# Attention and mixture of experts on one core: the experts' products in pairs

## The chip, the cores and the metric

The kernel runs on one core of one Trainium2 chip. The metric is device time in microseconds (us). Three runs of the kernel before took 2577.6, 2577.72 and 2578.16; the median is 2577.72.

## The reference

Everything is float32. The input x (4 x 1024 x 1024) is normalised per token to xn, and the result is the sum of x and two branches of xn:

```
x  = layernorm(x)                                    # xn
q, v = xn @ Wq, xn @ Wv                              # 16 heads
state[t] = sigmoid(beta) * state[t-1] + v[t]
y  = layernorm(q * state) * ln_g + ln_b
attn = (y * silu(xn @ Wg)) @ Wo                      # the projection

# 64 experts of 384 hidden units, 8 per token, at most 128 tokens each
h   = silu(xg[e] @ w1[e].T) * (xg[e] @ v1[e].T)      # xg[e]: 128 tokens gathered for e
ffn = scatter_add(weight * (h @ w2[e]))
out = x + attn + ffn
```

What changes is the order of the second half of the kernel, in which the 64 experts and the projection with Wo are computed. No value that is computed changes.

## The kernel before

The first half (to about 1232 us of the span) normalises, routes, scans and gates; it leaves the gated rows in DRAM (`gated`, 16 units of 256 rows), the tokens in `rows`, and x in the output `out`. The second half is `Experts.run`: a loop over 64 experts, with the projection's units cut into steps between them. The TensorE (PE) order, and that of VectorE (DVE) and ScalarE (ACT), is the order of the program there: `in_order(self.tc, ORDERED)` ties each instruction to the one before on its engine. SyncE (SP) issues loads and GpSimd (POOL) issues gathers and adds to `out`; each of these queues works through its own instructions in order, though a scheduler may place them earlier than the program text.

**Products of an expert, `hidden(e)`.** The hidden layer is a 2 x 2 block product done with seven block products (Winograd's form of Strassen's method). It needs sums of the left blocks (S1 to S4 in `s`, from `left_sums`, four additions of 128 x 256) and of the weights' blocks (T3, T1 by `sums31`, T2, T4 by `sums24`, each 128 x 1536; T1 is made in place in the weights). A block has 64 tokens, so the products use half of the PE array's columns, two at a time (`both`, with `tile_position` 0 or 64), in four groups:

1. into bank C, with S3 x T3 and S4 x B22,
2. into bank A, with A11 x B11 and S1 x T1,
3. into banks D and B, with S2 x T2 and A12 x B21,
4. into banks B and A, with A22 x T4 (half as long).

After each group ACT copies banks to SBUF and DVE adds them up in `q`, `up` and `act`; ACT applies silu, and DVE's last product leaves the hidden values in `act`. In between DVE makes the sums for the next expert and turns its gathered tokens (`turned`, a transpose from `xg` into `xgT`).

**Output of an expert.** `turn_hidden(e)` transposes `act` with three full-width matmuls into bank T, and ACT copies it to `hT`. `output(e)` computes y in two halves of 512 columns (banks D and T, three matmuls each), ACT scales them into a fresh tile `ys`, and POOL adds `ys` to the rows of `out` by an indirect DMA (L1001). The weights w2 of the expert (1.5 MB, one slot) are loaded by SP after the output before has used the slot.

**Steps of the projection, `steps`.** A unit has seven steps of four full-width matmuls each: step 1 into bank a (then an ACT copy), 2 into b, 3 into c (DVE adds b to the copy first, `c11`; ACT copies c), 4 adds to a (ACT copies it), 5 adds to c (DVE: `c12`, after which the row block `olo` is added to `out` by POOL), 6 adds to a (DVE: `c22`, L178, which reads bank a), 7 adds to a again (ACT copies it, and `ohi` is added to `out`). The projection's banks a, b and c are others than the experts' A, B and C. A unit's left factors come by `load_gated` and get their own `left_sums` on DVE; there is one place for them, so the next unit is loaded when step 7 has read it.

**The order.** For each expert e: `turn_hidden(e-1)`, `hidden(e)`, `output(e-1)`, then one or two steps, in the pattern 2, 2, 2, 1. So PE goes from full width to half columns and back once for each expert. The weights w and v of expert e+2 are loaded, and its tokens gathered, after `hidden(e)` (`fetch`). Each float32 matmul leaves two records in the trace, so a step is eight records and y twelve.

Of the kernel before, what the change touches and what calls it, by code (L numbers as in the profile page):

```python
# [39 lines left out]


NSLOT = 7


BLOCKS = ((0, 0), (1, 0), (1, 1), (0, 1))
# [774 lines left out]
class Experts:  # L820
# [8 lines left out]
    def load(self, e, n):  # L829


        if e >= E:
            return
        pools, (w, k) = self.pools, self.ws[n]
        slot = (n, e % 2) if n < 2 else (0, e % 2 ^ 1) if e == E - 1 else n
        if slot not in self.slots:
            t = (pools.x if e == 0 and n < 2 else pools.y)(f"w{n}_{e}")
            self.slots[slot] = t.rearrange("p a b -> p (a b)")
        t = self.slots[slot]
        done = self.nc.sync.dma_start(out=t, in_=w[e])  # L840
        if (e, n) == (1, 1):
            self.tc.keep_in_program_order(done)
        self.weights[e, n] = t.rearrange("p (k f) -> p k f", k=k)

    def fetch(self, e):

        for n in (1, 0):
            self.load(e, n)
        self.gather(e)

    def gather(self, e):
        if e >= E:
            return
        nc, pools = self.nc, self.pools
        if self.xg is None:
            self.xg = pools.block("xg").rearrange("p k (x c) -> p (k x) c", c=DQ)
        for r in range(NQ):
            nc.gpsimd.indirect_dma_start(  # L858
                out=self.xg[:, e % 2 * NQ + r, :],
                out_offset=None,  # L860
                in_=self.rows.rearrange("n (q c) -> (n q) c", q=NQ),
                in_offset=bass.IndirectOffsetOnAxis(ap=self.part[:, r, e : e + 1], axis=0),
            )
        nc.gpsimd.indirect_dma_start(
            out=self.wt[:, e % NQ, :],
            out_offset=None,
            in_=self.wtab,
            in_offset=bass.IndirectOffsetOnAxis(ap=self.idx[:, e : e + 1], axis=0),
        )

    def places(self):


        pools = self.pools
        t = pools.left.tile([P, NSLOT, KH, P], F32, tag="w", name="t23")
        t = t.rearrange("p a b c -> p (a b c)")
        u = pools.block("t4").rearrange("p a b -> p (a b)")
        n = KH * F
        self.t2, self.t3, self.t4 = (
            v.rearrange("p (k f) -> p k f", f=F) for v in (t[:, 0:n], t[:, n : 2 * n], u[:, 0:n])  # L880
        )
        self.p6, self.q = t[:, 2 * n : 2 * n + F], u[:, n : n + F]
        self.s = pools.one.tile([P, 4, KH, TH], F32, tag="cur", name="s")

    def turned(self, e):

        if e >= E:
            return
        xT = self.pools.line.tile([P, KD, P], F32, tag="line", name=f"xgT_{e}")
        done = self.nc.vector.transpose(  # L890
            xT.rearrange("p k (r i) -> p k r i", i=Q),
            self.xg[:, e % 2 * NQ : (e % 2 + 1) * NQ].rearrange("p r (k j) -> p k r j", j=Q),
        )
        if e == 0:
            self.tc.keep_in_program_order(done)
        self.xTs[e] = xT

    def left_sums(self, e):


        if e >= E:
            return
        vector = self.nc.vector
        a11, a12, a21, a22 = self.left_blocks(e)
        s1, s2, s3, s4 = (self.s[:, i] for i in range(4))
        vector.tensor_tensor(s3, a11, a21, ALU.subtract)
        vector.tensor_tensor(s1, a21, a22, ALU.add)
        vector.tensor_tensor(s2, s1, a11, ALU.subtract)
        vector.tensor_tensor(s4, a12, s2, ALU.subtract)

    def left_blocks(self, e):
        xT = self.xTs[e]
        return [xT[:, k : k + KH, i : i + TH] for i in (TH, 0) for k in (0, KH)]

    def right_blocks(self, e):

        return [self.weights[e, n][:, k : k + KH] for n in range(2) for k in (0, KH)]

    def sums31(self, e):

        if e < E:
            b11, _, b12, b22 = self.right_blocks(e)
            self.nc.vector.tensor_tensor(self.t3, b22, b12, ALU.subtract)  # L923
            self.nc.vector.tensor_tensor(b12, b12, b11, ALU.subtract)

    def sums24(self, e):
        if e < E:
            _, b21, t1, b22 = self.right_blocks(e)
            self.nc.vector.tensor_tensor(self.t2, b22, t1, ALU.subtract)  # L929
            self.nc.vector.tensor_tensor(self.t4, b21, self.t2, ALU.subtract)  # L930

    def hidden(self, e):


        nc, pools = self.nc, self.pools
        a11, a12, _, a22 = self.left_blocks(e)
        b11, b21, t1, b22 = self.right_blocks(e)
        s1, s2, s3, s4 = (self.s[:, i] for i in range(4))
        ba, bb, bc, bd = (self.banks[n][:, 0:F] for n in "ABCD")
        lo, hi = slice(0, TH), slice(TH, P)  # L940

# [12 lines left out]

        every, q, r, s = range(KH), self.q, self.act, self.p6
        both((bc, s3, self.t3, every), (bc, s4, b22, every))
        self.sums31(e + 1)
        both((ba, a11, b11, every), (ba, s1, t1, every))  # L960
        nc.scalar.copy(q, ba)
        nc.scalar.copy(r[lo], ba[hi])
        nc.scalar.copy(r[hi], ba[lo])
        nc.vector.tensor_tensor(q, bc, q, ALU.add)
        up = pools.scratch.tile([P, SH], F32, tag="sc", name=f"up_{e}")[:, 0:F]
        nc.vector.tensor_tensor(up, q, r, ALU.add)
        both((bd, s2, self.t2, every), (bb, a12, b21, every))
        nc.scalar.copy(s[hi], bd[lo])
        nc.scalar.copy(s[lo], bd[lo])
        nc.vector.tensor_tensor(up, up, s, ALU.add)  # L970
        nc.vector.tensor_tensor(q[lo], q[lo], s[lo], ALU.add)
        both((bb, a22, self.t4, (0, 1)), (ba, a22, self.t4, (2, 3)))
        nc.scalar.copy(r[lo], ba[hi])
        nc.vector.tensor_tensor(r, bb, r, ALU.add)
        nc.vector.tensor_tensor(r[lo], r[lo], q[lo], ALU.add)
        nc.scalar.activation(r, r, AF.Silu)
        self.turned(e + 1)
        nc.vector.tensor_tensor(r, r, up, ALU.mult)
        self.left_sums(e + 1)
        self.sums24(e + 1)  # L980
        for n in range(2):
            del self.weights[e, n]

    def turn_hidden(self, e):
        nc, pt = self.nc, self.banks["T"][:, 0:F].rearrange("p (j i) -> p j i", i=P)
        for j in range(KF):
            nc.tensor.transpose(pt[:, j, :], self.act[:, j * P : (j + 1) * P], self.ident)
        nc.scalar.copy(self.hT, pt)  # L988

    def output(self, e):  # L990
        nc, pools = self.nc, self.pools
        w2, wt, hT = self.weights.pop((e, 2)), self.wt[:, e % NQ, e : e + 1], self.hT
        ys = pools.line.tile([P, D], F32, tag="line", name=f"ys_{e}")
        for h, cols in enumerate((H0, H1)):
            ps = self.banks["DT"[h]]
            for j in range(KF):
# [45 lines left out]
    def begin(self, idx, part):  # L1042
        self.idx, self.part = idx, part
        v = self.pools.line.tile([P, S], F32, tag="line", name="act")
        self.act, self.hT = v[:, 0:F], v[:, F : 2 * F].rearrange("p (j i) -> p j i", i=P)
        self.wt = v[:, 2 * F :].rearrange("p (x e) -> p x e", e=E)
        self.fetch(0)

    def turn_first(self):
        self.places()  # L1050
        self.turned(0)
        self.left_sums(0)
        self.sums31(0)

    def run(self):
        nc, pools, units = self.nc, self.pools, B * NM
        self.banks = {n: pools.bank(tag, [P, SH], f"h{n}") for n, tag in zip("ABCDT", "abcrt")}
        with in_order(self.tc, [mybir.EngineType.SP]):
            self.load(1, 1)
            self.load_wo()  # L1060
            self.load(1, 0)
            gated = self.load_gated(0)
            self.load(0, 2)
        self.gather(1)
        wo_sums = right_sums(nc.vector, self.wo_b, lambda n: pools.block(f"wo_{n}"))


        plan = [(u, n) for u in range(units - 2) for n in (2, 2, 2, 1)]
        plan += [(units - 2, n) for n in (2, 2, 1, 1, 1)] + [(units - 1, 1)] * 3
        u, todo = -1, None  # L1070
        with in_order(self.tc, ORDERED):
            self.sums24(0)
            for _ in range(2):
                next(wo_sums)
            for e in range(E):
                if e > 0:
                    self.turn_hidden(e - 1)
                self.hidden(e)
                self.fetch(e + 2)
                if e == E - 2:  # L1080
                    self.load(E - 1, 2)
                if e == 0:
                    for _ in wo_sums:
                        pass
                else:
                    self.output(e - 1)
                    if e < E - 1:
                        self.load(e, 2)
                new, many = plan[e]
                if new > u:  # L1090
                    u, todo = new, self.project(new, gated)
                for _ in range(many):
                    next(todo, None)
                if e + 1 < E and plan[e + 1][0] > u:
                    gated = self.load_gated(u + 1)
            self.turn_hidden(E - 1)
            self.output(E - 1)
            for _ in todo:
                pass

# [47 lines left out]
```

## Time and profile before

| | |
|---|---|
| median of three runs | 2577.72 us |
| the profiled execution | 2577.84 us |
| its span, first to last instruction | 2576.1 us |
| granted TensorE clock | 0.999 |
| stage of experts and projection | about 1232 us to the end |
| DMA in all | 593.25 MB, of which SP's queue 448.03 and POOL's 143.72 |

The page of a profile lists the busy time of each engine, the busy shares over time, the DMA queues, the chain of work that ended last, and the costliest groups of instructions. A view by windows gives the same busy times for a stretch, with the share of time in which the 16 DMA engines were busy. The timeline lists single instructions or merged runs of them by start and duration; in brackets stands the idle time before one and what ended it. A matmul's duration in these records overlaps the next one's, so the distance of two starts is what a matmul costs.

### The profile page before, as it was taken

Reading aid. Unit: us, or ns where it says so; the run is one execution under the profiler, and the core shown is the slowest. Engines: PE = TensorE matmul, PEld = TensorE weight load, DVE = VectorE, ACT = ScalarE, POOL = GpSimd, SP = SyncE. Lnnn points to the kernel's source line nnn. Section 1 sums busy time; section 2 is a strip of 40 time slices with the busy share of each in tenths; the row PEclk is TensorE's granted clock in tenths of the full one; section 3 lists DMA queues with packets and bytes.
Section 4 is the critical chain, followed back from the end, with each engine's and each line's share of the span. In section 5 each row is a group of like instructions: output and inputs, shape, how many; then the busy total and the mean of one; then the engine's idle time right before and its main releaser. Section 6 shows DMA issues by size and latency. Waiting matters only on the chain.

```text
span 2576.1 us, 23153 instructions
## 1 busy us (share of the span) xinstructions
PE 2558.7 (99%) x8453; PEld 1132.6 (44%) x8453; DVE 1707.2 (66%) x2116; ACT 616.1 (24%) x1048; POOL 855.5 (33%) x630
## 2 busy tenths in 40 slices
PE   9999999999999999999999999999999999999998
PEld 5444444444444444444444444444444444444443
DVE  7946677375954668347866666666676666766673
ACT  4112212131111310112222222222222222222222
POOL 1452302101022010322344444444444444444441
PEclk9999999999999999999999999999999999999999
DMA  5655625543345442235899888898989899888995
GB/s 186 259 171 216 200 78 182 185 129 120 118 151 196 143 143 86 100 126 204 296 312 307 287 298 306 310 306 284 326 300 311 284 319 307 301 297 288 318 339 119
DMA packets 122354, 593.25 MB, mean 230 GB/s; under 512 B 15856, under 2 KB 52720, under 8 KB 89216
## 3 DMA queue, kind: packets, MB, share of 16 engines
q1 hardware_dynamic: 81488, 448.03, 47.0%
q0 software_dynamic: 40320, 143.72, 20.8%
q8 instruction: 67, 1.10, 0.2%
q14 instruction: 47, 0.39, 0.0%
q10 hardware_dynamic: 432, 0.01, 0.0%
HBM read 483.67 MB, written 124.81 MB: 236 GB/s over the span
## 4 chain that ended last, share of the span: by engine, by line
PE 95%; DVE 4%; issue 0%; DMA 0%; ACT 0%; POOLq 0%; SPq 0%; DVEq 0%
PE pa_g L143 9%; PE pa_o L143 8%; PE pa_q L143 7%; PE pa_v L143 7%; PE hD L997 7%; PE hC L946 7%; PE hA L946 7%; PE hT L997 6%; PE hD L946 6%; PE pc_o L143 4%; PE pc_g L143 4%; PE pc_v L143 4%; PE pc_q L143 4%; PE hB L946 3%; PE pb_o L143 2%; PE pb_g L143 2%
## 5 line engine op out<-in xcount | busy, mean ns | idle before, releaser
L858 POOL DMA_INDIRECT xg<-rows,tables x256 | 390.8, 1527 | 426.7 <-DVE xgT L890 363.3
L923 DVE TENSOR_TENSOR t<-w 128x1536 f32<-128x1536 f32 x64 | 112.5, 1758 | 236.7 <-PE hC L946 226.6
L143 PE MATMUL pa_g<-xT,w 128*128 128x512 f32 x512 | 230.8, 593 | 0.0
L143 PE MATMUL pa_q<-xT,w 128*128 128x512 f32 x480 | 216.6, 593 | 4.0 <-DVE y L178 4.0
L143 PE MATMUL pa_v<-xT,w 128*128 128x512 f32 x480 | 215.8, 592 | 0.0
L997 PE MATMUL hD<-w,act 128*128 128x512 f32 x384 | 181.9, 610 | 0.8 <-ACT act L988 0.7
L946 PE MATMUL hC<-t,s 128*64 128x384 f32 x512 | 179.1, 492 | 0.0
L946 PE MATMUL hC<-w,s 128*64 128x384 f32 x512 | 179.0, 492 | 0.0
L946 PE MATMUL hA<-w,xgT 128*64 128x384 f32 x512 | 175.6, 486 | 0.0
L946 PE MATMUL hD<-t,s 128*64 128x384 f32 x512 | 175.6, 486 | 0.0
L946 PE MATMUL hA<-w,s 128*64 128x384 f32 x512 | 175.6, 486 | 0.0
L946 PE MATMUL hB<-w,xgT 128*64 128x384 f32 x512 | 175.6, 486 | 0.0
L997 PE MATMUL hT<-w,act 128*128 128x512 f32 x384 | 175.2, 592 | 0.0
L143 PE MATMUL pa_o<-wo_T,gated 128*128 128x512 f32 x384 | 172.7, 592 | 0.8 <-DVE ohi L178 0.8
L691 POOL DMA_DIRECT2D gated<-y x64 | 48.6, 764 | 325.7 <-DVE y L686 315.4
L143 PEld LDWEIGHTS pa_g<-xT,w 128*128 128x128 f32 x512 | 96.8, 190 | 122.8 <-issue 121.8
L1001 POOL DMA_INDIRECT out_dram<-ys,tables x64 | 112.6, 1760 | 110.3 <-issue 49.5
L143 PEld LDWEIGHTS pa_q<-xT,w 128*128 128x128 f32 x480 | 90.5, 190 | 117.0 <-issue 109.8
L143 PEld LDWEIGHTS pa_v<-xT,w 128*128 128x128 f32 x480 | 91.1, 190 | 115.0 <-issue 110.0
L930 DVE TENSOR_TENSOR t<-w,t 128x1536 f32<-128x1536 f32 x64 | 112.5, 1759 | 7.4 <-DVE t L929 0.5
L143 PE MATMUL pc_g<-xT,w 128*128 128x512 f32 x256 | 115.7, 592 | 0.0
L143 PE MATMUL pc_q<-xT,w 128*128 128x512 f32 x256 | 115.5, 593 | 0.0
(245 smaller groups left out, 4414.9 us busy)
## 6 DMA issues: line engine op xcount, KB each, us to landing
w<-in_w_dram SPq DMA_DIRECT2D x128, 1536.0 KB
w<-in_v_dram SPq DMA_DIRECT2D x64, 1536.0 KB
w<-wsum SPq DMA_DIRECT2D x36, 1792.0 KB
wsum<-w POOLq DMA_DIRECT2D x12, 1792.0 KB
x<-in_x_dram SPq DMA_DIRECT2D x32, 512.0 KB
rows<-x POOLq DMA_DIRECT2D x32, 512.0 KB
gated<-y POOLq DMA_DIRECT2D x64, 256.0 KB
gated<-gated SPq DMA_DIRECT2D x16, 1024.0 KB
```

The costliest lines, as they stand in the source:

```text
L143: nc.tensor.matmul(ps, lhsT=lhs[:, slot, k, :], rhs=blocks[right][:, k, :], start=start and k == 0, stop=stop and k == KH - 1, skip_group_ ...
L691: nc.gpsimd.dma_start(out=gated[b, :, :, slot, m, :].rearrange("u p j -> p u j"), in_=yc[:, h * SH : (h + 1) * SH].rearrange("p (u j) -> p ...
L858: nc.gpsimd.indirect_dma_start(out=self.xg[:, e % 2 * NQ + r, :], out_offset=None, in_=self.rows.rearrange("n (q c) -> (n q) c", q=NQ), in ...
L923: self.nc.vector.tensor_tensor(self.t3, b22, b12, ALU.subtract)
L930: self.nc.vector.tensor_tensor(self.t4, b21, self.t2, ALU.subtract)
L946: nc.tensor.matmul(bank[half], lhsT=a[:, ks[k], :], rhs=b[:, ks[k], :], start=(k == 0), stop=(k == len(ks) - 1), tile_position=(0, half.st ...
L997: nc.tensor.matmul(ps, lhsT=hT[:, j, :], rhs=w2[:, j, cols], start=(j == 0), stop=(j == KF - 1))
L1001: nc.gpsimd.indirect_dma_start(out=self.out, out_offset=bass.IndirectOffsetOnAxis(ap=self.idx[:, e : e + 1], axis=0), in_=ys, in_offset=No ...
```

## The change

The experts are taken in groups: expert 0 alone, then pairs (1, 2), (3, 4) up to (61, 62), then 63 alone. In a group the products of both experts come first, one `hidden` after the other. Then for each expert of the group in turn: its transposes, one or two steps of the projection (`between`), and its y. Some groups have steps ahead of the first transposes (`ahead`) or at the end (`behind`). To have two experts at once, `s`, `act` and `xgT` have two places each; `ys` and `up` have one place for all experts. The transposes go into bank D instead of T. Within a pair the second expert's weight sums are made during the first's products, one by one (`right_sum`); those for the next group's first expert follow between the transposes and y. w2 is loaded in two halves of its columns, each as soon as y has used that half of the slot. The weight column `wt` has eight places. Gathers run four experts ahead.

```
+    def right_sum(self, e, n):
+        if e >= E:
+            return
+        b11, b21, b12, b22 = self.right_blocks(e)
+        to, a, b = {
+            3: (self.t3, b22, b12),
+            1: (b12, b12, b11),
+            2: (self.t2, b22, b12),
+            4: (self.t4, b21, self.t2),
+        }[n]
+        self.nc.vector.tensor_tensor(to, a, b, ALU.subtract)
...
     def load(self, e, n):
...
+        if n == 2:
+            from_ = w[e].rearrange("p (k f) -> p k f", k=k)
+            for cols in (H0, H1):
+                self.nc.sync.dma_start(out=t[:, :, cols], in_=from_[:, :, cols])
+            return
...
+    def more_places(self):
+        pools = self.pools
+        t = pools.line.tile([P, S], F32, tag="line", name="s1")
+        self.s[1] = t.rearrange("p (i k c) -> p i k c", i=4, k=KH)
+        self.ys = pools.line.tile([P, D], F32, tag="line", name="ys")
+        t, u = (pools.scratch.tile([P, SH], F32, tag="sc", name=n) for n in ("act1", "up"))
+        self.acts[1], self.up = t[:, 0:F], u[:, 0:F]
...
-    def hidden(self, e):
+    def hidden(self, e, turn, then_next):
...
-        self.sums31(e + 1)
+        if then_next:
+            for n in (3, 1):
+                self.right_sum(e + 1, n)
...
+        if then_next:
+            self.right_sum(e + 1, 2)
         both((bb, a22, self.t4, (0, 1)), (ba, a22, self.t4, (2, 3)))
...
-        self.turned(e + 1)
+        self.turned(turn)
         nc.vector.tensor_tensor(r, r, up, ALU.mult)
-        self.left_sums(e + 1)
-        self.sums24(e + 1)
+        if then_next:
+            self.right_sum(e + 1, 4)
...
     def turn_hidden(self, e):
-        nc, pt = self.nc, self.banks["T"][:, 0:F].rearrange("p (j i) -> p j i", i=P)
+        nc, pt = self.nc, self.banks["D"][:, 0:F].rearrange("p (j i) -> p j i", i=P)
...
     def run(self):
...
             self.load(1, 1)
             self.load_wo()
+            self.load(0, 2)
+            gated = self.load_gated(0)
             self.load(1, 0)
-            gated = self.load_gated(0)
-            self.load(0, 2)
...
+        plan = [((0,), 2, (1,), 0), ((1, 2), 0, (1, 2), 1)]
+        plan += [((e, e + 1), 0, (1, 2), e // 2 % 2) for e in range(3, last - 4, 2)]
+        plan += [((e, e + 1), 0, (1, 1), 0) for e in (last - 4, last - 2)]
+        plan += [((last,), 1, (0,), 0)]
...
+            for group, ahead, between, behind in plan:
+                new = group[-1] + 1
+                for e in group:
+                    self.hidden(e, e + 2 if e else 1, e != group[-1])
+                    for n in (1, 0):
+                        self.load(e + 2, n)
+                    if e == last - 1:
+                        self.load(last, 2)
+                    if e == group[0]:
+                        self.gather(e + 4 if e else 3)
+                project(ahead)
+                for i, e in enumerate(group):
+                    self.turn_hidden(e)
+                    project(between[i])
+                    if i == 0:
+                        if e == 0:
+                            for _ in wo_sums:
+                                pass
+                            self.turned(2)
+                        for n in (0, 1):
+                            self.left_sums(new + n)
+                        for n in (3, 1):
+                            self.right_sum(new, n)
+                    self.output(e)
+                    if e + 1 < last:
+                        self.load(e + 1, 2)
+                    if i == 0:
+                        self.gather(group[-1] + 4)
+                    if e == group[-1]:
+                        for n in (2, 4):
+                            self.right_sum(new, n)
+                project(behind)
```

`project(n)` here runs the next n steps of the projection, starts the next unit when one is done, and issues its load.

More of the change, by code (lines that the diff above doesn't have):

```diff
@@ L42 @@
 NSLOT = 7
+NWT = 8
 BLOCKS = ((0, 0), (1, 0), (1, 1), (0, 1))
@@ L838, in load @@
             self.slots[slot] = t.rearrange("p a b -> p (a b)")
-        t = self.slots[slot]
-        done = self.nc.sync.dma_start(out=t, in_=w[e])
+        t = self.weights[e, n] = self.slots[slot].rearrange("p (k f) -> p k f", k=k)
+        if n == 2:
[3 more added lines that the diff above has]
+            return
+        done = self.nc.sync.dma_start(out=self.slots[slot], in_=w[e])
         if (e, n) == (1, 1):
             self.tc.keep_in_program_order(done)
[L843 to L849, printed above, removed]
     def gather(self, e):
@@ L864, in gather @@
         nc.gpsimd.indirect_dma_start(
-            out=self.wt[:, e % NQ, :],
+            out=self.wt[:, e % NWT, :],
             out_offset=None,
@@ L882, in places @@
         self.p6, self.q = t[:, 2 * n : 2 * n + F], u[:, n : n + F]
-        self.s = pools.one.tile([P, 4, KH, TH], F32, tag="cur", name="s")
+        self.s = {0: pools.one.tile([P, 4, KH, TH], F32, tag="cur", name="s")}
+    def more_places(self):
[5 more added lines that the diff above has]
+        self.acts[1], self.up = t[:, 0:F], u[:, 0:F]
     def turned(self, e):
@@ L888, in turned @@
             return
-        xT = self.pools.line.tile([P, KD, P], F32, tag="line", name=f"xgT_{e}")
+        if e < 2:
+            self.xTs[e] = self.pools.line.tile([P, KD, P], F32, tag="line", name=f"xgT_{e}")
+        xT = self.xTs[e % 2]
         done = self.nc.vector.transpose(
@@ L895, in turned @@
             self.tc.keep_in_program_order(done)
-        self.xTs[e] = xT
     def left_sums(self, e):
@@ L904, in left_sums @@
         a11, a12, a21, a22 = self.left_blocks(e)
-        s1, s2, s3, s4 = (self.s[:, i] for i in range(4))
+        s1, s2, s3, s4 = (self.s[e % 2][:, i] for i in range(4))
         vector.tensor_tensor(s3, a11, a21, ALU.subtract)
@@ L911, in left_blocks @@
     def left_blocks(self, e):
-        xT = self.xTs[e]
+        xT = self.xTs[e % 2]
         return [xT[:, k : k + KH, i : i + TH] for i in (TH, 0) for k in (0, KH)]
@@ L917, in right_blocks @@
         return [self.weights[e, n][:, k : k + KH] for n in range(2) for k in (0, KH)]
[L919 to L930, printed above, removed]
-    def hidden(self, e):
-        nc, pools = self.nc, self.pools
+    def right_sum(self, e, n):
[10 more added lines that the diff above has]
+    def hidden(self, e, turn, then_next):
+        nc = self.nc
         a11, a12, _, a22 = self.left_blocks(e)
         b11, b21, t1, b22 = self.right_blocks(e)
-        s1, s2, s3, s4 = (self.s[:, i] for i in range(4))
+        s1, s2, s3, s4 = (self.s[e % 2][:, i] for i in range(4))
         ba, bb, bc, bd = (self.banks[n][:, 0:F] for n in "ABCD")
@@ L953, in both @@
                     )
-        every, q, r, s = range(KH), self.q, self.act, self.p6
+        every, q, r, s, up = range(KH), self.q, self.acts[e % 2], self.p6, self.up
         both((bc, s3, self.t3, every), (bc, s4, b22, every))
-        self.sums31(e + 1)
+        if then_next:
+            for n in (3, 1):
+                self.right_sum(e + 1, n)
         both((ba, a11, b11, every), (ba, s1, t1, every))
@@ L964, in hidden @@
         nc.vector.tensor_tensor(q, bc, q, ALU.add)
-        up = pools.scratch.tile([P, SH], F32, tag="sc", name=f"up_{e}")[:, 0:F]
         nc.vector.tensor_tensor(up, q, r, ALU.add)
@@ L984, in turn_hidden @@
     def turn_hidden(self, e):
-        nc, pt = self.nc, self.banks["T"][:, 0:F].rearrange("p (j i) -> p j i", i=P)
+        nc, pt = self.nc, self.banks["D"][:, 0:F].rearrange("p (j i) -> p j i", i=P)
         for j in range(KF):
-            nc.tensor.transpose(pt[:, j, :], self.act[:, j * P : (j + 1) * P], self.ident)
+            nc.tensor.transpose(pt[:, j, :], self.acts[e % 2][:, j * P : (j + 1) * P], self.ident)
         nc.scalar.copy(self.hT, pt)
     def output(self, e):
-        nc, pools = self.nc, self.pools
-        w2, wt, hT = self.weights.pop((e, 2)), self.wt[:, e % NQ, e : e + 1], self.hT
-        ys = pools.line.tile([P, D], F32, tag="line", name=f"ys_{e}")
+        nc, ys, hT = self.nc, self.ys, self.hT
+        w2, wt = self.weights.pop((e, 2)), self.wt[:, e % NWT, e : e + 1]
         for h, cols in enumerate((H0, H1)):
@@ L1044, in begin @@
         v = self.pools.line.tile([P, S], F32, tag="line", name="act")
-        self.act, self.hT = v[:, 0:F], v[:, F : 2 * F].rearrange("p (j i) -> p j i", i=P)
-        self.wt = v[:, 2 * F :].rearrange("p (x e) -> p x e", e=E)
-        self.fetch(0)
+        self.acts = {0: v[:, 0:F]}
+        self.hT = v[:, F : 2 * F].rearrange("p (j i) -> p j i", i=P)
+        self.wt = self.pools.small.tile([P, NWT, E], F32, tag="sel", bufs=1, name="wt")
+        for n in (1, 0):
+            self.load(0, n)
+        self.gather(0)
     def turn_first(self):
@@ L1052, in turn_first @@
         self.left_sums(0)
-        self.sums31(0)
+        for n in (3, 1):
+            self.right_sum(0, n)
     def run(self):
@@ L1060, in run @@
             self.load_wo()
+            self.load(0, 2)
+            gated = self.load_gated(0)
             self.load(1, 0)
-            gated = self.load_gated(0)
-            self.load(0, 2)
-        self.gather(1)
+        for e in (1, 2):
+            self.gather(e)
         wo_sums = right_sums(nc.vector, self.wo_b, lambda n: pools.block(f"wo_{n}"))
-        plan = [(u, n) for u in range(units - 2) for n in (2, 2, 2, 1)]
-        plan += [(units - 2, n) for n in (2, 2, 1, 1, 1)] + [(units - 1, 1)] * 3
@@ L1070, in run, with project @@
-        u, todo = -1, None
+        last = E - 1
+        plan = [((0,), 2, (1,), 0), ((1, 2), 0, (1, 2), 1)]
+        plan += [((e, e + 1), 0, (1, 2), e // 2 % 2) for e in range(3, last - 4, 2)]
+        plan += [((e, e + 1), 0, (1, 1), 0) for e in (last - 4, last - 2)]
+        plan += [((last,), 1, (0,), 0)]
+        todo, u, left = None, 0, 0
+        def project(n):
+            nonlocal todo, u, left, gated
+            for _ in range(n):
+                if left == 0:
+                    todo, left = self.project(u, gated), NSLOT
+                next(todo, None)
+                left -= 1
+                if left == 0:
+                    u += 1
+                    gated = self.load_gated(u) if u < units else None
@@ L1071, in run @@
         with in_order(self.tc, ORDERED):
-            self.sums24(0)
+            for n in (2, 4):
+                self.right_sum(0, n)
             for _ in range(2):
                 next(wo_sums)
[L1075 to L1095, printed above, removed]
@@ L1096, in run @@
-            self.turn_hidden(E - 1)
-            self.output(E - 1)
+            self.more_places()
+            for group, ahead, between, behind in plan:
+                new = group[-1] + 1
+                for e in group:
+                    self.hidden(e, e + 2 if e else 1, e != group[-1])
+                    for n in (1, 0):
+                        self.load(e + 2, n)
[14 more added lines that the diff above has]
+                            self.left_sums(new + n)
+                        for n in (3, 1):
+                            self.right_sum(new, n)
[5 more added lines that the diff above has]
+                    if e == group[-1]:
+                        for n in (2, 4):
+                            self.right_sum(new, n)
+                project(behind)
```

## The prediction

> **What bounds the kernel now.** I read the table of cores first (one core, 2576.1 us, granted clock 0.999, so no throttling), then the busy table and the chain of waits, then one window of the expert stage.
>
> ```profile
> PE 2558.7 (99%) x8453; PEld 1132.6 (44%) x8453; DVE 1707.2 (66%) x2116; ACT 616.1 (24%) x1048; POOL 855.5 (33%) x630
> PE 95%; DVE 4%; issue 0%; DMA 0%; ACT 0%; POOLq 0%; SPq 0%; DVEq 0%
> 1500.00:2000.00 500.00, 499.90 (x2036) 219.88 (x2034) 341.86 (x426) 138.44 (x264) 231.23 (x156) 1.00 0.89 304
> ```
>
> PE is never idle in the stage that changes (499.90 of 500), and the chain is 95% PE. So a microsecond added to or taken from PE's sequence is a microsecond of the kernel. The last two columns matter as well: the DMA engines are 0.89 busy at 304 GB/s, so transfers have little room to bunch.
>
> "Busy" hides the spacing of the matmuls, which the timeline of PE shows (start, duration, engine, line, tile):
>
> ```profile
> 1704.32 3.60 PE L143 MATMUL pa_o<-wo_T,gated 128*128 128x512 f32 x8
> 1707.75 0.49 PE L987 MATMUL hT<-ident,act 128*128 128x128 f32 x3
> 1708.17 0.54 PE L946 MATMUL hC<-t,s 128*64 128x384 f32 x1
> ...
> 1708.55 0.49 PE L946 MATMUL hC<-t,s 128*64 128x384 f32 x1
> ...
> 1708.87 0.49 PE L946 MATMUL hC<-t,s 128*64 128x384 f32 x1
> ...
> 1716.93 0.49 PE L946 MATMUL hB<-t,xgT 128*64 128x384 f32 x1
> ...
> 1717.35 2.84 PE L997 MATMUL hD<-w,act 128*128 128x512 f32 x6
> 1720.03 2.74 PE L997 MATMUL hT<-w,act 128*128 128x512 f32 x6
> 1722.61 3.60 PE L143 MATMUL pa_o<-wo_T,gated 128*128 128x512 f32 x8
> ```
>
> Half-column products start every 0.323 us, full-width matmuls every 0.429, transposes every 0.109. At the seam into half columns the last transpose takes 0.202 instead of 0.109 (+0.093), and the first product 0.374 instead of 0.323 (+0.051). At the seam out, the last product takes 0.416 instead of 0.316 (+0.100), and the first six matmuls of y take 2.68 instead of 2.58 (+0.105). One visit to half columns thus costs **0.349 us**; an expert with one step takes 18.29 us, of which the matmuls alone explain 17.94.
>
> **Part 1, experts in pairs.** The two orders of PE show 65 entries into half columns before and 34 after, so 31 visits go: 31 x 0.349 = 10.8 us. The seam out now meets a 128-column transpose. No row shows it; between nothing saved and the whole 0.105 saved on the 33 groups (0 to 3.5 us), I take half, as at the seam in (0.051): 1.6. Together **-12.4**.
>
> Does the pair hold without gaps? With hidden() of the first expert at 0, its groups start at 0, 2.6, 5.2, 7.8 and end at 9.1; the second's run from 9.1 to 18.2. DVE, by the rows of L923 to L978: T3 and T1 of the second expert from 2.8 to 6.4, adds, T2 at 10.0 to 11.7 (needed at 14.3), last adds and the transpose, T4 at 14.3 to 16.1 (needed at 16.9). That fits, with 0.8 us to spare. ACT copies hT of the first expert after the second's silu, at 20.8 to 21.3; one step of the projection (18.7 to 22.1) lies over it, so y starts at 22.1 without a wait. Cost nothing; without that step 2.6 us a pair.
>
> **Part 2, the steps between.** The plan now does 1 and 2 (and 1 behind) in one pair, 1 and 2 in the next. The order of PE shows what this makes of the seven steps: (1 | 2,3 | 4), then (5 | 6,7). Steps 6 and 7 both use bank a: step 7 may accumulate only when VectorE has read step 6's sum (L178). Before, an expert's products stood between them, except in the tail, which shows the price:
>
> ```profile
> 2560.38 3.60 PE L143 MATMUL pa_o<-wo_T,gated 128*128 128x512 f32 x8
> 2564.76 3.70 PE L143 MATMUL pa_o<-wo_T,gated 128*128 128x512 f32 x8 [0.79 <-DVE ohi L178]
> 2564.01 0.69 DVE L178 TENSOR_TENSOR ohi<-pa_o,sc_o 128x512 f32<-128x512 f32 x1 [2.67 <-PE pa_o L143]
> ```
>
> Eight matmuls at 0.429 are 3.43; the distance is 4.38, so 0.95 lost. VectorE is free in time (by my timetable its sums end at 29.7, step 6 at 31.2), so no more is lost. The order has 15 such neighbours, 1 before: 14 x 0.95 = **+13.3**. Behind the waiting matmul stand y and everything after; nothing passes it.
>
> **Part 3, the start.** Expert 0 stays alone. Between its products and those of expert 1, VectorE now has, after 1243.4: left sums of gated (2.5), the add after step 2 (ends 1247.9), two sums of Wo (rows L70, L73: 4.5), a transpose (1.2), eight left sums (3.1), T3 (1.8): 1258.5. PE gets there at 1255.9 (transposes 1247.0, 0.33, a step 3.43, y 5.14). Wait 2.6; T1, T2, T4 then chase it, some 0.3 more: **+2.9** (0 to 4). On SP the load of w for expert 1 moves behind w2 and gated into the slot whose last store ends near 1241; at the 0.43 MB a microsecond that the queue moves when alone it has landed by about 1250, and T1 reads it at 1258: nothing. The gather of the weight column moves behind the ys add and is used two pairs later: nothing.
>
> **Part 4, one place for ys; w2 in halves.** PE's own work is unchanged, but two transfers get deadlines.
>
> ys: ScalarE may write y of the second expert (at 38.2) only when the scatter-add of the first has landed, and PE feels it when bank D is not free for the next pair's third group (45.8, so landing by 45.0). The adds onto out wait for each other:
>
> ```profile
> POOL out_dram L1029 <- DMA out_dram<-ys,tables: 44.1, 10, 8.3
> POOL out_dram L1001 <- DMA out_dram<-ohi: 27.7, 7, 4.3
> ```
>
> In the second pair of each unit POOL issues both gathers (until about 29), then the projection's row block, then ys. By the trace's landing events from 1300 to 2500, a row block lands 12.0 us (olo) or 10.6 us (ohi) after issue, ys 6.8 (median; 13.7 at the 90th percentile): 29.1 + 12.0 + 6.8 = 47.9, 2.9 too late, 14 times: 41 us. The Trainium skill (DMA: Bandwidth & Descriptors, "Anatomy of one DMA — SWDGE (gpsimd) path") fits such a transfer by 2.0 us plus bytes over 436e3: 3.2 us for 512 KB. With 1.6 us for each issue both land by 38.7, and the wait is nothing. In the tail, with idle queues, the trace has 4.6 (olo) and 5.4 (ys), giving 39. The 12.0 was measured behind fresh 12 KB packets of w and v (0.46 us each); here 2 KB packets of w2 (0.084 us) compete, so I go nearer to the tail: 0.5 us x 14 = **+7**.
>
> w2: the second expert's halves are issued when the first expert's y lets go (25 and 27.5), queued behind w and v of the expert after next (issued at 14.6 and 17.2 on the same SP queue), and needed at 34.5 and 37.1. In the window, v took 7.4 us to land, w 10.8 (so until about 28) and a whole w2 8.6, beside the gathers. From 28, two halves of 2.0 us of engine time, sharing with the adds, land between 31 and 36. Between no wait and 1.5 us I take 0.4 x 14 = **+6**. The load of gated has 20 us before its use.
>
> **Tail.** Same work, one step before the last transposes; they wait 0.2 longer for VectorE: +0.2.
>
> **Sum**: -12.4 + 13.3 + 2.9 + 0.2 = +4.0, with the transfers +17. The profiled execution took 2577.84 us (span 2576.1 and 1.7 around it; the median is 2577.72, so nothing needs shifting): **2595 us**.
>
> **Rivals.**
> - *The transfers stay hidden* (not slower). Place: bank D and the w2 halves; price nothing as long as ys lands within 16.8 us of the end of the gathers and a half within 9.5 of its issue. For it: every PE wait on DMA is zero now, and the tail's landings. Against it: 0.89 busy and the adds' serial order. Then +4.0: 2582, inside 0.2%.
> - *Step 7's wait is absorbed* (faster): 2577.8 - 12.4 + 2.9 + 0.2 = 2568. For it only that 14 waits were extrapolated from one; against it, nothing follows on PE that could slide in.
> - *The transfers pace the stage*: per pair the engines need 4 x 3.7 (w, v), 4 x 2.05 (halves), 1.3, gathers 5.2, adds 7.8, some 37 of 41.5 us; w and v of a pair cannot start before its second group and the queue runs dry there. At 1.5 us a pair over 31 pairs, 46 more: 2628.
>
> **How the numbers follow.** The forecast has 0.55, hidden transfers 0.25, paced by transfers 0.16, faster 0.04. This kernel's runs tell 0.2% (5.2 us) from no change. Of the 0.25, two thirds stay within that: same 0.17, slower 0.55 + 0.16 + 0.08 = 0.79. Range 2579 to 2613: it leaves out the faster case and the lowest hidden ones (0.08), and most of the paced ones (0.12).
>
> **What will show it.** Right: PE's group of pa_o with 14 more waits of 0.8 on DVE ohi; entries 31 fewer, at 0.35 each; one gap of some 2.6 near 1256; waits of PE on DMA for w2 or of ScalarE ys on the DMA of ys. Wrong: PE idle in the stage clearly under 13 us, or a first transpose dearer than 0.1 after the products, or a gap in the pair at T4 (0.8 us spare).

## The result, and the profile after

The changed kernel took 2610.96 us (median of 4 runs, 2608.14 to 2612.41), the kernel before, on the same chip, 2577.94. The ratio is 1.0127, with a 95% interval of 1.0109 to 1.0144: slower by 33 us. The forecast was slower, 2595, range 2579 to 2613. The side is right, the range holds the time, and the number is 16 us too low.

The profiled execution of the changed kernel spans 2608.6 us, 32.5 more than before. Its page, from the parts on busy time and on the costliest groups:

```profile
PE 2557.6 (98%) x8453; PEld 1129.9 (43%) x8453; DVE 1705.8 (65%) x2116; ACT 612.7 (23%) x1048; POOL 777.6 (30%) x630
...
L144 PE MATMUL pa_o<-wo_T,gated 128*128 128x512 f32 x384 | 174.2, 596 | 11.8 <-DVE ohi L179 11.8
...
L1011 PE MATMUL hT<-w,act 128*128 128x512 f32 x384 | 176.0, 594 | 6.3 <-DMA w<-in_w_dram 6.2
L958 PE MATMUL hC<-t,s 128*64 128x384 f32 x512 | 177.5, 489 | 2.5 <-DVE t L940 2.4
```

TensorE was busy for about as long as before (2557.6 us against 2558.7), so by the page's rows the 32.5 us are idle time. The window from 1500 to 2000, in which TensorE had been busy for 499.90, shows it with the DMA engines still at 0.90 of their time:

```profile
1500.00:2000.00 500.00, 488.77 (x2007) 214.18 (x2007) 331.41 (x410) 133.28 (x257) 192.18 (x149) 1.00 0.90 297
```

The view of waits says for whom TensorE idled (engine, line, tile, what it waited for: us in all, times, longest):

```profile
PE hD L1002 <- ACT ys L1014: 12.0, 5, 3.3
PE pa_o L144 <- DVE ohi L179: 11.8, 15, 0.8
PE hT L1011 <- DMA w<-in_w_dram: 6.2, 5, 2.6
...
PE hC L958 <- DVE t L940: 2.4, 1, 2.4
```

These rows understate: a matmul lasts 0.592 us in the records but costs 0.429, so each wait hides 0.16 of itself, and the second matmul after a wait starts 0.105 late (0.534 for 0.429; called the refill below). Taken from the distances of starts of all TensorE's matmuls in both traces, each against its undisturbed distance, the span's difference falls into these parts:

| part | forecast, us | measured, us |
|---|---|---|
| 31 fewer visits to half columns | -12.4 | -11.9 |
| step 7 waits for step 6 (bank a) | +13.3 | +14.7 |
| the start, near 1256 | +2.9 | +2.8 |
| one place for ys | +7 | +14.6 |
| half TensorE clock behind two of these waits | none | +3.5 |
| halves of w2 late | +6 | +8.1 |
| tail, last matmul to the end included | +0.2 | +0.5 |
| sum | +17 | +32.3 of 32.5 |

The largest miss is the place for ys. This is POOL's timeline in one pair (start, duration, what it issues, and in brackets the idle time before it):

```profile
2225.32 1.00 POOL L1043 DMA_DIRECT2D out_dram<-olo  x1
2234.76 1.62 POOL L1015 DMA_INDIRECT out_dram<-ys,tables  x1 [8.44 <-issue]
...
2244.59 0.95 POOL L1043 DMA_DIRECT2D out_dram<-ohi  x1 [6.89 <-DVE t L940]
2256.98 1.61 POOL L1015 DMA_INDIRECT out_dram<-ys,tables  x1 [11.44 <-issue]
```

ScalarE's timeline has what these adds hold up, and TensorE's what ScalarE holds up:

```profile
2244.07 0.69 ACT L1014 ACTIVATE ys<-hD,wt 128x512 f32<-128x512 f32 x1 [9.07 <-DMA out_dram<-ys,tables]
...
2269.52 0.69 ACT L1014 ACTIVATE ys<-hD,wt 128x512 f32<-128x512 f32 x1 [7.05 <-DMA out_dram<-ys,tables]
```

```profile
2264.26 2.74 PE L1011 MATMUL hT<-w,act 128*128 128x512 f32 x6
2270.26 0.77 PE L1002 MATMUL hD<-ident,act 128*128 128x128 f32 x3 [3.26 <-ACT ys L1014]
2270.82 5.11 PE L144 MATMUL pb_o<-wo_B,gated 128*128 128x512 f32 x8
```

Read it as one chain: the row block olo goes out at 2225.3, the first ys at 2234.8 (9.4 later, when olo has landed), ohi at 2244.6 (9.8), the second ys at 2257.0 (12.4), and that lands at 2269.5 (12.5): four adds in single file, 44 us in a pair of 42. ScalarE may not overwrite ys before. The second expert's write (2244.07) comes all but in time for bank D (0.14 us are lost there). The next pair's first write comes at 2269.52, and the transposes that want bank D stand for 3.26 us. The trace has six such stops, of 1.5 to 3.4 us each, in 14 pairs of this kind.

The adds tell the six from the other eight. The same four adds in a pair without a stop:

```profile
1884.89 1.01 POOL L1043 DMA_DIRECT2D out_dram<-olo  x1
1894.49 1.62 POOL L1015 DMA_INDIRECT out_dram<-ys,tables  x1 [8.59 <-issue]
1902.64 0.95 POOL L1043 DMA_DIRECT2D out_dram<-ohi  x1 [5.22 <-DMA out_dram<-ys,tables]
1910.28 2.06 POOL L1015 DMA_INDIRECT out_dram<-ys,tables  x1 [6.69 <-issue]
```

From ohi to the second ys are 7.6 us here and 12.4 above. Over the 14 pairs this distance is 10.8 to 12.9 us in the six that stop and 6.7 to 9.3 in the eight that do not. Why ohi takes longer to land in the six is open.

In TensorE's last line above, the step behind the stop takes 5.11 us where 3.60 is usual; more on this at the end.

### The profile page after: what moved, and what is told of

It reads as the page before. It is cut to its first block, busy times and chain, and to the rows that moved or that the text cites. A ratio compares the mean times of both kernels' runs of the same rounds, so it can differ in the third digit from the quotient of the medians.

```text
span 2608.6 us, 23232 instructions
## 1 busy us (share of the span) xinstructions
PE 2557.6 (98%) x8453; PEld 1129.9 (43%) x8453; DVE 1705.8 (65%) x2116; ACT 612.7 (23%) x1048; POOL 777.6 (30%) x630
## 5 line engine op out<-in xcount | busy, mean ns | idle before, releaser
L940 DVE TENSOR_TENSOR t<-w 128x1536 f32<-128x1536 f32 x128 | 224.0, 1750 | 288.3 <-PE hC L958 285.5
L858 POOL DMA_INDIRECT xg<-rows,tables x256 | 308.0, 1203 | 298.7 <-DVE xgT L901 224.9
L1011 PE MATMUL hD<-w,act 128*128 128x512 f32 x384 | 175.3, 592 | 0.6 <-ACT act L1003 0.6
L1011 PEld LDWEIGHTS hT<-w,act 128*128 128x128 f32 x384 | 72.4, 190 | 100.5 <-issue 87.3
```

Source lines behind the costliest of these rows:

```text
L858: nc.gpsimd.indirect_dma_start(out=self.xg[:, e % 2 * NQ + r, :], out_offset=None, in_=self.rows.rearrange("n (q c) -> (n q) c", q=NQ), in ...
L940: self.nc.vector.tensor_tensor(to, a, b, ALU.subtract)
L1011: nc.tensor.matmul(ps, lhsT=hT[:, j, :], rhs=w2[:, j, cols], start=(j == 0), stop=(j == KF - 1))
```

## Experiments

Each time is a median with its ratio to the kernel before in the same session (2577.4 to 2578.2).

**Steps 6 and 7 apart, in the changed kernel.** The two patterns of a unit change places.

```
-        plan += [((e, e + 1), 0, (1, 2), e // 2 % 2) for e in range(3, last - 4, 2)]
+        plan += [((e, e + 1), 0, (1, 2), (e // 2 + 1) % 2) for e in range(3, last - 4, 2)]
```

> The changed kernel with the two step patterns of a unit swapped, so that the seven steps fall as (1 | 2,3), then (4 | 5,6 | 7), and steps 6 and 7 are no longer neighbours. Theory (each lost stretch of TensorE is a cost of its own): the 15 distances of 1.376 us between step 6 and step 7 fall back to 0.429, 14 x 0.947 = 13.3 us go, from 2611 to about 2598; the waits for ys and for w2 stay within some 6 us of what they are, since the adds onto out are only put in another order. Rival (the transfers pace the stage): what is taken from the wait on bank a comes back as waits for ys or w2, and the time stays at 2608 to 2613.

Measured: 2581.47 us (20 runs, 2574.89 to 2587.43), ratio 1.0014 (1.0007 to 1.0021). That is 29.5 below the changed kernel, where the theory had 13.3 and the rival none. The waits of TensorE:

```profile
PE hD L1011 <- DMA w<-in_w_dram: 4.7, 8, 2.0
...
PE hC L958 <- DVE t L940: 2.4, 1, 2.4
PE hT L1011 <- DMA w<-in_w_dram: 2.3, 5, 0.8
...
PE pa_o L144 <- DVE ohi L179: 0.8, 1, 0.8
```

The 14 waits on bank a are gone, and so is every wait for ys, which I had expected to stay. The adds now come as ys, olo, ys, ohi: one row block less stands before the second ys, and ohi has the next pair's products to land in. By distances: 14.7 for bank a, 18.1 for ys and its half clock, less 3.4 by which the w2 waits grew (8.1 to 11.5), makes 29.4 of 29.5. (Later expectations take the w2 waits of this run from its rows, 4.7 + 2.3 = 7.0; by distances they are 11.5.) The rival has fallen.

**The same neighbours in the kernel before.**

```
-        plan = [(u, n) for u in range(units - 2) for n in (2, 2, 2, 1)]
+        plan = [(u, n) for u in range(units - 2) for n in (2, 2, 1, 2)]
```

> The kernel before with the steps of a unit dealt (2, 2, 1, 2) over four experts in place of (2, 2, 2, 1), so that steps 6 and 7 become neighbours and nothing else changes. Theory: 14 more distances of 1.38 us in place of 0.43, +13.3 us, 2591. Rival (the wait belongs to the late order of VectorE in the pairs, not to the neighbours): VectorE has finished step 6's sum in the gap anyhow or the wait is made good later, and the time stays within 2 us of 2578.

Measured: 2592.13 us, ratio 1.0058 (1.0041 to 1.0075): +14.75. Its trace has the row of the changed kernel to the tenth, and no wait for a transfer:

```profile
L143 PE MATMUL pa_o<-wo_T,gated 128*128 128x512 f32 x384 | 174.2, 596 | 11.8 <-DVE ohi L178 11.8
```

14 x (0.947 + 0.105) = 14.7. So this cost belongs to the neighbours alone, and the forecast's 13.3 lacked the refill after each wait.

**The adds of the projection later, in the changed kernel.** They go into a list, and one is issued behind the ys of a pair's second expert.

```
         def add(o, h):
-            nc.gpsimd.dma_start(out=self.out[r0 : r0 + P, :], in_=o, accum_op=ALU.add)
+            to = self.out[r0 : r0 + P, :]
+            self.adds.append(lambda: nc.gpsimd.dma_start(out=to, in_=o, accum_op=ALU.add))
...
                     if e == group[-1]:
+                        if self.adds:
+                            self.adds.pop(0)()
```

> The changed kernel in which the projection's adds onto out are issued later: each waits in a list and one is issued after the ys of a pair's second expert, so that a pair has three adds at most and none stands between the first ys and the second, or between the last ys of one pair and the first of the next, except the one. Theory (ScalarE's write of ys waits because the two row blocks and two scatter-adds of one pair land one after the other): the six losses of 1.5 to 3.9 us at the first expert's ys go, with the two stretches of half clock behind the longest, together some 15 to 18 us, from 2611 to about 2594; the wait on bank a and the w2 waits stay. Rival (the DMA engines are full and the order of the adds does not matter): the waits for ys become as many waits for w2 or stay, 2608 to 2613.

Measured: 2594.04 us, ratio 1.0074 (1.0057 to 1.009), 17 below the changed kernel, where the theory had 15 to 18 and the rival 3 at most. TensorE's waits are those of bank a and a few of w2; none is for ys:

```profile
PE pa_o L144 <- DVE ohi L179: 11.8, 15, 0.8
...
PE hT L1013 <- DMA w<-in_w_dram: 2.4, 3, 1.1
...
PE hD L1013 <- DMA w<-in_w_dram: 0.8, 1, 0.8
```

The same bytes moved through the same queue, so it was the order and spacing of the adds. By distances the waits for w2 fall too, from 8.1 to some 4.3 us, and the list's rest at the end lengthens the tail by 3.2. A second place for ys, the direct test of this wait, was not run.

**A visit more in each second pair.** On top of the swapped patterns, step 4 stands between the products of the two experts.

```
+                split = len(group) == 2 and behind == 1 and group[0] > 1
                 for e in group:
+                    if split and e == group[1]:
+                        project(1)
                     self.hidden(e, e + 2 if e else 1, e != group[-1])
...
-                    project(between[i])
+                    project(1 if split else between[i])
```

> The swapped patterns of the run before this one, and in every second pair (4 | 5,6 | 7) step 4 stands between the products of the two experts: 14 more visits to half columns. Theory (a visit costs 0.349 us of TensorE, and TensorE bounds the stage): 14 x 0.35 = +4.9 us over the run with the patterns swapped alone. Rival (the transfers pace the stage, or the price of a visit is an overlap that is regained): +0, as 4.9 us of TensorE hide behind waits.

Measured: 2631.9 us, ratio 1.0205 (1.0188 to 1.0222): 50 above the swapped run, a miss for both theories. The chain of waits has the visit at its price: the step between takes 3.63 where 3.43 is usual, and the group of products after it 2.73 for 2.58, together 0.35. Then the same chain has this:

```profile
1698.31 3.63 PE pa_o L144 x8
1701.93 2.73 PE hC L958 x16
...
1711.59 3.44 PE pc_o L144 x8
1715.03 2.58 PE hD L1011 x6
1717.60 2.58 PE hT L1011 x6
1720.21 8.86 DMA w<-in_w_dram
1729.11 2.84 PE hT L1011 x6
```

The second half of w2's place comes free at 1720.2, and its next content lands 8.86 us later. Between the two y stands one step instead of two, so the half is wanted after some 6 us. I had moved a step without seeing that it was the time in which a half of w2 could land. In all, the waits for w2 are 43.7 us by the rows, where the swapped run has 7.0:

```profile
PE hT L1011 <- DMA w<-in_w_dram: 38.1, 17, 3.7
PE hD L1011 <- DMA w<-in_w_dram: 5.6, 10, 1.2
```

Most of the rest is 4.9 for the visits and, by an estimate from the distances (six times 1.6), some 10 for half TensorE clock behind six of the waits (last section).

**Two trials to bring w2 earlier.** The first gives the halves to ScalarE's queue, with and without the step between the products:

```
-                self.nc.sync.dma_start(out=t[:, :, cols], in_=from_[:, :, cols])
+                (self.nc.scalar if e else self.nc.sync).dma_start(out=t[:, :, cols], in_=from_[:, :, cols])
```

> The swapped patterns, with the halves of w2 issued from ScalarE's queue in place of SP's, behind ScalarE's write of ys. Theory (a half comes late because it stands in one queue behind w and v of the expert after next): the waits of y for w2, 7.0 us in the profile of the swapped run, go, from 2581.5 to about 2574.5, so faster than before by some 3 us. Rival (the DMA engines are full, and any order of the transfers takes as long): 2581 within 2 us, with the waits moved to w or to ys.

> The swapped patterns with step 4 between the products of the two experts in every second pair, and w2 from ScalarE's queue. In the run with SP's queue this step cost 50 us, 37 of them in waits for w2's halves. Theory (the step delays the second expert's products, and so w and v, and so the halves queued behind these, while y comes earlier; the visit itself costs 0.349 us): with w2 out of that queue only the visits are left, +4.9 us over the run with swapped patterns and ScalarE's queue, near 2579.5. Rival (the engines' share is what is short): still 30 to 50 us over it.

Measured: 2614.9 (1.0139, 1.0118 to 1.0159) and 2656.34 (1.0305, 1.0288 to 1.0323): 33 and 75 above the swapped run. For the first, both theories missed; the second lies 41 above the first, as its rival had it. ScalarE's timeline says why this was no test of the queue alone:

```profile
1723.27 0.69 ACT L1014 ACTIVATE ys<-hD,wt 128x512 f32<-128x512 f32 x1 [9.14 <-DMA out_dram<-ys,tables]
1725.85 0.69 ACT L1014 ACTIVATE ys<-hT,wt 128x512 f32<-128x512 f32 x1 [1.89 <-PE hT L1011]
1725.87 1.27 ACTq L844 DMA_DIRECT2D w<-in_w_dram  x2
```

Both halves now leave together behind the second write of ys, 2.6 us later for the first half, and behind any wait of ScalarE for ys. The median from issue to landing is 7.6 us, and TensorE's waits for w2 are 31.5 and 3.8:

```profile
PE hT L1011 <- DMA w<-in_w_dram: 31.5, 24, 2.9
```

The second trial keeps SP's queue and puts w of the second next expert behind the halves (SP's instructions are also tied to the order of the program; the swapped run's trace has its weight loads in that order already):

```
-                    for n in (1, 0):
+                    for n in (1, 0) if e == group[0] else (1,):
                         self.load(e + 2, n)
...
                         self.load(e + 1, 2)
+                    if i < len(group) - 1:
+                        self.load(group[1] + 2, 0)
```

> The swapped patterns, with one transfer moved on SP's queue: w of the pair's second next expert is issued behind the two halves of w2 for the second expert in place of ahead of them. Theory (a half is late because SP's queue first empties 3 MB of w and v: in the swapped run its first packet moves 3.5 us after its issue and its last 8.3, where 9.8 us are there): each half lands some 3 us earlier, the 7.0 us of waits for w2 go, from 2581.5 to about 2575. Rival (the engines are short of time, whatever the order): w2 is in time and w is late at VectorE's sums, 2581 or above.

> As the run with w moved, and step 4 between the products of the two experts in every second pair. With SP's queue as it was, this step cost 50 us: one step between the two y leaves a half of w2 some 6.3 us from issue to use, and it lands after 8. Theory: with w out of the way a half lands after some 5, and most of the 50 us go; what stays is 15 visits at 0.35, 5 us, and up to 10 of waits, 2580 to 2590. Rival (a half needs 8 us in any order): near 2625.

Measured: 2586.38 (15 runs; 1.0032, 1.0022 to 1.0041) and 2628.55 (1.02, 1.0183 to 1.0217). Without the extra step, w2 does come earlier, and the gain does not follow. Counted by packets of the trace, the later half for a pair's second expert has its last packet 5.5 us after issue (median, 8.3 in the swapped run), and TensorE waits once for w2. Instead it waits for ys:

```profile
PE hD L958 <- ACT ys L1014: 13.3, 7, 2.6
...
PE hT L1011 <- DMA w<-in_w_dram: 1.6, 1, 1.6
```

These are waits of the third group of products for bank D, the very place at which the prediction put the ys wait. By distances, some 10 us of w2 were exchanged for 14.5 of ys. The rival had the time (2581 or above) but another place, w at VectorE's sums. Why ys is late in this order was not tested. With the step between the products, that half of w2 still has its last packet 7.7 us after issue and the waits are 35.2: there the rival holds.

**w2 whole.**

```
-            for cols in (H0, H1):
-                self.nc.sync.dma_start(out=t[:, :, cols], in_=from_[:, :, cols])
+            self.nc.sync.dma_start(out=t, in_=from_)
```

> The swapped patterns with w2 of an expert as one transfer in place of two halves by columns. Theory (the halves let the first half leave 2.6 us earlier, and a whole w2 issued when the second half of its place is free has 7.2 us until its first use, against 5 to 8 us that one took to land in the kernel before): waits for w2 grow from 7 us to some 20 to 40, 2595 to 2615. Rival (halves only add packets, of 2 KB in place of 12): the same or less, 2575 to 2581.

Measured: 2605.57, ratio 1.0108 (1.0091 to 1.0125): 24 above the swapped run, as the theory had it. The w2 of a pair's second expert lands 7.1 to 8.1 us after issue (median 7.5), and 7.0 are there before y has to wait:

```profile
L1010 PE MATMUL hD<-w,act 128*128 128x512 f32 x384 | 182.0, 611 | 23.0 <-DMA w<-in_w_dram 21.3
```

TensorE's waits for w2 are three times those of the swapped run by the rows (21.3 and 7.0), so the halves are a gain within the pairs, though they raise the packets from 122353 to 164338.

**The start.** VectorE's sums T2 and T4 of Wo move behind work that the products of experts 1 and 2 need; tried first with w2 on ScalarE's queue, with and without the later adds, then on SP's queue with w moved, where T2 stands earlier.

> The swapped patterns, w2 from ScalarE's queue, and at the start VectorE's sums T2 and T4 of Wo (4.5 us) moved behind the sums that the second expert's products need. Theory (the one gap near 1256 is VectorE's order): that gap, 2.5 us with what chases it, goes; 2.5 us below the run without it, near 2572. Rival (VectorE is as late one expert on): the same 2.5 us come back in the first pair, 2574.5.

> As the run before this one, and the projection's adds are issued later, one behind each pair's second ys. Theory (after the swap no ys waits any more): nothing is left for the later adds to win, 2572 within 2 us. Rival (the adds also crowd w, v and w2): up to 3 us less.

> As the run before this one, and at the start VectorE does the sum T2 of Wo behind T4 of expert 1 and the sum T4 of Wo behind the sums of the first pair. Theory: the gap of 2.5 us near 1256 goes and some 1.2 us come back at the first product of expert 2, whose bank waits for an add behind the 2.3 us of that sum: 1 to 1.5 us below the run before. Rival: VectorE's lateness is only handed on, 0.

The first two leave out expert 2: its gathered rows are overwritten before VectorE turns them, so those of expert 4 are turned twice. They do as much work, so their times are shown, but they do not compute the same result. Measured: 2617.01 (1.0147, 1.013 to 1.0164), 2610.36 (1.0124, 1.0107 to 1.0141) and 2580.8 (12 runs; 1.0012, 1.0003 to 1.0021). The gap near 1256 went in all three. In the first two it came back larger, since T2 was behind all sums of the pair: step 4 waited 5.2 us for it. In the third, some 2.1 us came back (0.44 at a product of expert 2, 1.46 at a step behind T4, and the refill after each), so the start itself gave 0.7. The median lies 5.6 us below the run without it, and the runs of either kernel spread over 10 us or more. The two profiled executions (2576.43 and 2585.58) differ most in the waits for ys, three in place of seven (5.1 us for 13.3). Why there are fewer, and whether this holds for the medians, is open. The later adds were worth 6.7 us beside ScalarE's queue, against nothing by the theory and 3 at most by the rival: the waits for w2, which ScalarE issues behind its writes of ys, fall from 35.1 to 26.7 us.

No version was faster than the kernel before. The swapped patterns with w moved *and* the adds issued later were not tried together; from the parts, the waits that each leaves are those which the other removes, but the trial of w2's order showed how such sums can go.

## Why the prediction was right, and where it was not

**The bound** was right: TensorE's sequence sets the time, and other engines show only where TensorE stops for them. All but 0.2 of the 32.5 us are found as a gap or a price on TensorE.

**The visits** were right: -12.4 forecast, -11.9 measured. The seam onto the transposes saves about half of the 0.105, as chosen: the first distance between transposes is 0.165 in place of 0.109, so 0.056 of it stays. (The seam is met 31 times, not 33: experts 0 and 63 have steps ahead of their transposes.) The pair itself holds without a gap.

**Step 7** was right in mechanism and count, and 1.4 short: each wait costs 0.947 and 0.105 more at the second matmul after it. The row to see that from stood in the prediction's own fence: 3.70 beside 3.60 for the matmuls behind the wait. The rival that the wait is absorbed fell with the run on the kernel before.

**The start** was right: 2.9 and 2.8.

**The place for ys** is the term that was mis-sized: 7 forecast, 14.6 measured and 3.5 of clock behind it. The step that failed is "2 KB packets of w2 compete, so I go nearer to the tail". It took the long landings of the trace before (12.0, 10.6) as the work of 12 KB packets, discounted them and chose a sixth of the sum that they gave (41 us). For olo and the first ys together the long rows had 18.8 us, the tail 10.0. In the trace after, 17.5 to 19.3 us lie between the issue of olo and that of ohi, which waits for this ys: near the long rows in every one of the 14 pairs. In the pair shown the four adds take 9.4, 9.3 from issue to landing of the first ys, 12.4 and 12.5. The 41 were still too many, since 6 pairs of the 14 stop and not all. The estimate of 3.2 us by the fit of the Trainium skill (DMA: Bandwidth & Descriptors, "Anatomy of one DMA — SWDGE (gpsimd) path") is three to four times too short for these four adds. The place was off as well: the prediction saw the second expert's write late, at bank D in the next pair's products, but followed the chain of adds only to that point. The second expert's own add is late as well then, and it hits the first expert of the next pair, which the prediction did not look at. Only with w moved did the foreseen place decide.

**The halves of w2** were right in place, and 2 short (6 and 8.1): six stops of 0.3 to 2.8 us, not 14 of 0.4.

**The rivals.** "Hidden transfers" (2582) is what the swapped patterns reach, by another road: they take the wait on bank a away and still wait for w2. "The transfers pace the stage" (2628) is wrong for this change as a whole, since of bank a's and ys's waits only 3.4 us came back at w2. It is right in the small: past the swapped patterns, the one trial that brought w2 in time made ys late. The range held by 2 us. Its upper end of 2613 was set by how much of this rival to leave out, not by a larger ys term, so that it held is in part luck. What was not foreseen is that one line of the plan decides both the wait on bank a and the order of the adds, 29.5 us of the 33.

## What to carry to other kernels

When two consumers share one output by read-modify-write, list their adds in issue order and lay the trace's own landing times, under load and not from the tail, end to end over one period. If the sum comes near the period, a single buffer before them can stop the engine that fills it. Look at each of its writes: here the stop showed one add later than where the chain first got tight, and in another order of the loads at that first place. A change of order should be priced with everything that rides on it: here the places of seven small steps set a PSUM wait, the order of four adds, and the time a weight has to land.

## What the runs showed of the hardware that was not expected

**The clock after a wait.** Behind some waits TensorE ran at half rate, 0.853 us a matmul instead of 0.429, for some 3 to 4 us in the trace after. The view by windows has the granted clock in the third column from the end, here behind the wait of 2.76 us that ends at 1415.81 (a distance of 3.36) and behind that of 3.26 (3.85):

```profile
1417.00:1421.00 4.00, 4.00 (x7) 1.65 (x6) 0.00 (x0) 0.00 (x0) 3.08 (x4) 0.57 0.85 306
...
2270.00:2273.50 3.50, 3.24 (x7) 1.70 (x8) 0.57 (x1) 1.26 (x3) 2.89 (x3) 0.56 1.05 377
```

It costs about 1.7 us each time, half as much again as the distance lost. It does not follow the length alone. Distances of 3.23 and 3.62 in the same trace had none. In the run with the step between the products on SP's queue one of 2.46, with 1.86 us idle, had it, and two of 3.3 had not. The first line here is behind the distance of 3.62, the second behind that of 2.46:

```profile
2528.10:2531.60 3.50, 3.50 (x11) 1.52 (x10) 3.43 (x3) 0.79 (x2) 2.91 (x1) 1.00 0.82 304
1815.50:1819.00 3.50, 3.50 (x5) 1.62 (x6) 0.00 (x0) 0.00 (x0) 1.87 (x2) 0.57 1.04 277
```

The Trainium skill (TensorE: Matmul & The Clock Gate, "Part 1: The HAM clock gate") has a free-running window of about 3.4 us, after an idle one of which the clock is halved. A window that runs free fits waits of one length that differ. But 1.86, 2.76 and 3.26 us idle are all less than a whole window, and this is not explained by it. In none of the traces was a distance under 2.46 followed by half rate.

**Two halves in one queue.** With w2 on ScalarE's queue, the first packets of the first half moved 1.4 us after issue (median, pair's second expert; 3.3 on SP's queue, where w and v are ahead of it). Those of the later half, issued together with the first, moved after 3.8 us (3.5 on SP's queue), most of the 4.9 us that the first half takes to its last packet. So the later half stood behind the first one in its queue. Since the issue moved too, what the other queue is worth by itself was not separated.
